# First attention layer's window phase: the next layer's group norm by ScalarE squares with sums and GpSimd two-operation pieces

## The chip, the cores and the metric

The kernel runs on one core of a Trainium2 chip. The metric is the device time of one execution in microseconds (us). TensorE is called PE in the profile, VectorE DVE, ScalarE ACT, GpSimd POOL; SP issues the DMAs.

## The reference

Four images of 256 channels and 64x64 positions pass through four layers, each added to its own input. Layers 0 and 1 are attention layers, layers 2 and 3 are state-space (Mamba) layers. Every layer's input is first normalised in 32 groups:

```python
def _gn(v, G=32, eps=1e-5):
    B_, H_, W_, C_ = v.shape
    g = v.reshape(B_, H_, W_, G, C_ // G)
    m = jnp.mean(g, axis=(1, 2, 4), keepdims=True)
    s = jnp.var(g, axis=(1, 2, 4), keepdims=True)
    return ((g - m) / jnp.sqrt(s + eps)).reshape(v.shape)
...
x = x + L0(_gn(x))   # attention
x = x + L1(_gn(x))   # attention
x = x + L2(_gn(x))   # state space
x = x + L3(_gn(x))   # state space
```

(The last four lines are shortened.) Since the array is (image, channel, row, column), its last axis, the image column, plays the part of the channel, and a group is two neighbouring columns. So a norm needs the mean and the variance of pairs of columns over all channels and rows.

An attention layer runs a gated recurrence along one image axis (the scan phase), cuts the result into 64 windows of 8x8, picks for each window the four windows with the most similar mean, and attends with 8 heads from the window's 64 queries to the 256 keys of those four (the window phase). A depthwise 3x3 convolution of the values ("lepe") is added, and a 1x1 projection gives the layer's output.

## The kernel before

One image at a time: `net_kernel` loops over four images ("batches" here), keeps the image x in SBUF as 128 partitions by 8192 fp32 values (two halves of channels), runs both attention layers in `attention_layers` and then the two state-space layers.

The attention layers cut the image into eight strips of eight columns, which is four norm groups per strip. A strip's slice of x is read as (channel half, column, row): neighbouring elements of that order lie 64 values apart in x, because columns are innermost in memory. All order within a phase is the order of the program text (`manual_schedule`): each engine runs its own instructions in that order, and waits for the others where data or a buffer demands it.

The norm of one strip has two forms.

- `gn` (L125) makes the normalised strip in seven steps: sums of x by DVE, a small product on PE that adds over channels, `center` (a DVE copy of the mean, then a GpSimd subtraction of 128x1024 into a buffer with tag "xn", L151), `square` (one ScalarE instruction of 128x1024 into a buffer with tag "sq", L156), `reduce` (a DVE sum of 128x1024, L160), a small product, and `scale` (a small DVE add, a GpSimd power, L168, and a GpSimd multiply of 128x1024 in place, L172).
- `stats` (L189) makes only the variances, for the state-space layer that follows layer 1: sums, product, negative mean, four ScalarE squares of 128x256 straight from x with the mean as bias and the sum accumulated by the same instruction (L215), product, and a small copy.

Tag "xn" has two buffers, tag "sq" has one. The one "sq" buffer also holds the products of the convolution's taps where GpSimd does them: `weigh` (L254) multiplies a shifted image by a weight into it, and `add` (L257) adds it to the value image. Each is one step, and GpSimd runs one such step per pair.

The window phase (`window_phase`, L477) loops over 32 pairs of windows. Pair i has two halves h of the heads. Per half: `scores` (PE, L546), `smallest` (DVE, L558), `exps` (four ScalarE instructions with accumulated sums, L569), `normalise` (a DVE reciprocal, L581, and four GpSimd multiplies of 128x256, L584), `turn` (eight PE transposes, L597), `turned` (one copy on DVE, L608, one on ScalarE, L610), `values` (PE, L623), and once per pair `own_rows` (a DVE add of the pair's outputs, L634). The halves and pairs are interleaved: pair i's loop body transposes the second half of pair i-1 and makes the first scores of pair i+1. In two pairs of every four, `project` adds a 1x1 projection into a finished strip of x (DVE, L644). `gather` issues the key and value loads for pair i+3 on SP's queue.

Other work is hung into this loop by two tables, `mids` and `ends`: steps under `mids[i]` run in the middle of pair i, before `normalise(i, 0)`; those under `ends[i]` at its end, behind the pair's tap. In layer 0 these are the norms of layer 1's first two strips, strip s in pairs 7+4s to 12+4s; in layer 1 they are the `stats` of strips 0 to 6:

```python
if nxt:
    load_scan_weights(nxt)
    for s in range(2):
        i = 7 + 4 * s
        plan(gn(nxt, s, lambda: psum), (ends, i), (ends, i + 1), (mids, i + 2),
             (ends, i + 3), (mids, i + 4), (ends, i + 4), (mids, i + 5))
```

Layer 1's scan phase reads the two normalised strips as the input of its first products (`conv_ps<-att_xn`).

Of the kernel before, what the change touches and what calls it, by code (L numbers as in the profile page):

```python
# [8 lines left out]
F32 = mybir.dt.float32  # L9
# [3 lines left out]
ALU = mybir.AluOpType  # L13
# [5 lines left out]
P = 128  # L19
# [4 lines left out]
NW = 8  # L24
# [20 lines left out]
class Net:  # L45
# [33 lines left out]
    def attention_layers(self, x, w_drams, v_drams):  # L79
        tc, nc = self.tc, self.nc  # L80
        with ExitStack() as ctx:
# [31 lines left out]
            def load_scan_weights(lay):  # L113
                lay["wa"] = wp.tile([P, 2, 4 * C], F32, tag="wa", name="att_wa")
                nc.sync.dma_start(lay["wa"], lay["w"][:, :, 0 : 4 * C])
# [70 lines left out]
                return g[0], both(g[1], g[2]), both(g[3], g[4]), both(g[5], g[6])  # L186


            def stats(s, psum):  # L189
                xs = x.rearrange("p (c h w) -> p c w h", c=2, w=S)[:, :, strip[s], :]  # L190
                box = {}

                def columns(tag, part):
                    box[tag] = psum().tile([P, NT], F32, tag="mm", name=f"gn_{tag}")
                    nc.tensor.matmul(box[tag][:, 0:4], self.one_gn, part, start=True, stop=True)

                def sums():
                    box["s1"] = self.small.tile([P, 4], F32, tag="gn_s1", name="gn_s1")
                    xr = x.rearrange("p (n w) -> p n w", w=S)[:, :, strip[s]]
                    nc.vector.tensor_reduce(  # L200
                        box["s1"], xr.rearrange("p n (g t) -> p g n t", t=2), AX.XY, ALU.add
                    )

                def mean():
                    box["mean"] = self.small.tile([P, 4], F32, tag="gn_mean", name="gn_mean")
                    nc.vector.tensor_scalar(
                        box["mean"], box["pm"][:, 0:4], -1.0, None, ALU.mult
                    )

                def square(g):  # L210
                    if g == 0:
                        box["s2"] = self.small.tile([P, 4], F32, tag="gn_s2", name="gn_s2")
                        box["sq"] = norm.tile([P, 2, 8, S], F32, tag="xn", name="gn_sq")
                    two = slice(2 * g, 2 * g + 2)
                    nc.scalar.activation(  # L215
                        box["sq"][:, :, two], xs[:, :, two], AF.Square,
                        bias=box["mean"][:, g : g + 1], accum_out=box["s2"][:, g : g + 1],
                    )

                def variance():  # L220
                    nc.vector.tensor_copy(self.gvar[:, 4 * s : 4 * s + 4], box["pv"][:, 0:4])  # L221

                return (
                    sums, lambda: columns("pm", box["s1"]), mean,
                    *(lambda g=g: square(g) for g in range(4)),
                    lambda: columns("pv", box["s2"]), variance,
                )


# [247 lines left out]
            def window_phase(lay, work, psum, idx, nxt, taps):  # L477
# [13 lines left out]
                def load_row():  # L491
                    listed = dram.tile([NW * NW, 8], U32, tag="listed", name="listed")
                    nc.sync.dma_start(listed, idx)
                    nc.sync.dma_start(
                        row.rearrange("o (s a) k -> o s a k", a=NW),
                        listed[:, 0:TOPK].rearrange("(o a s) k -> o s a k", o=1, a=NW),
                    )
# [37 lines left out]
                def scores(i, h):  # L535
                    sj, a = divmod(i, 4)
                    if i < n_pair:
                        sc[h] = psum.tile([P, 2, 2, 2, P], F32, tag="sc", name="sc", bufs=2)
                        for w in range(2):
                            for m in range(2):  # L540
                                for b in range(2):
                                    for r in range(2):
                                        r0 = r * 64 + h * 32
                                        rows = slice(r0, r0 + 32)
                                        k0 = b * P + m * 64
                                        nc.tensor.matmul(  # L546
                                            sc[h][b * 64 : b * 64 + 64, r, w, m, :],
                                            (own(sj, m) if r == b else swap[sj % 2][:, m])[
                                                rows, 2 * a + w
                                            ],  # L550
                                            kv[i, w][rows, :, k0 : k0 + 64],
                                            start=True, stop=True,
                                        )
# [98 lines left out]
                for i in range(3):  # L652
                    gather(i)
                    indices(i + 1)
                load_row()
                scores(0, 0)
                scores(0, 1)
                early = [query(lay, 5, m, psum, nc.vector, tag="pt", bufs=2) for m in range(2)]
# [5 lines left out]
                mids, ends, left = {}, {}, []  # L664

                def plan(steps, *where):
                    for f, (at, i) in zip(steps, where):
                        if i < n_pair:
                            at.setdefault(i, []).append(f)
                        else:  # L670
                            left.append(f)

                if nxt:
                    load_scan_weights(nxt)
                    for s in range(2):
                        i = 7 + 4 * s
                        plan(gn(nxt, s, lambda: psum), (ends, i), (ends, i + 1), (mids, i + 2),
                             (ends, i + 3), (mids, i + 4), (ends, i + 4), (mids, i + 5))
                else:

                    for s in range(NW - 1):
                        i = 4 * s + 7
                        plan(stats(s, lambda: psum), (ends, i), (ends, i + 1), (mids, i + 2),
                             (ends, i + 2), (mids, i + 3), (ends, i + 3), (mids, i + 4),
                             (ends, i + 4), (mids, i + 5))
                for i in range(n_pair):
                    sj, a = divmod(i, 4)
                    add = evict = None
# [63 lines left out]
                box = {}  # L752
# [3 lines left out]
            with tc.tile_pool(name="at_p0", bufs=2, space=PSUM, reuse_waits="tile") as psum:  # L756
                box = {"psum": psum}
                g = [gn_four(layers[0], s, lambda: box["psum"]) for s in range(2)]
# [3 lines left out]
            for i, lay in enumerate(layers):  # L762
                with tc.tile_pool(name=f"at_a{i}", bufs=1, reuse_waits="tile") as work, tc.tile_pool(
                    name=f"at_p{i}", bufs=5, space=PSUM, reuse_waits="tile"
# [1407 lines left out]
```

## Time and profile before

| | |
|---|---|
| median of 3 runs | 11914.07 us (11912.61 to 11917.38) |
| profiled execution | 11903.13 us, span 11901.3 us, mean granted TensorE clock 0.932 |
| PE busy | 10069.9 us (85%) |
| DVE busy | 9868.8 us (83%) |
| POOL busy | 8695.6 us (73%) |
| ACT busy | 7006.9 us (59%) |

In the profile a row such as "L156 ACT ACTIVATE gn_sq<-att_xn 128x1024 x64: 1046/1056/1057" is one group of instructions: source line, engine, operation, output and inputs, shape, number, and the shortest, median and longest duration in ns. Timeline rows begin with the start and the duration in us; the square brackets give the time for which the engine sat idle before the row, and what released it. Rows of windows begin with a stretch of time and its length, then the busy time of each engine with its number of instructions, then the TensorE clock that was granted (1.00 is full speed), the share of time that the DMA engines were busy, and what they moved.

### The profile page before, as it was taken

To read this page: it belongs to the slowest core of one execution; us is meant where nothing else is said; L and a number is where in the kernel's file an instruction comes from. 1 tells how busy PE (TensorE), PEld (TensorE's weight loads), DVE (VectorE), ACT (ScalarE), POOL (GpSimd) and SP (SyncE) were. 2 spreads that over 40 slices of the span, in tenths; PEclk is the share of its full clock that TensorE was granted. 3 is DMA by queue.
4 is the path that set the end of the run, shared out by engine and by line. 5 is a ranking of instruction groups with operands and counts; after the bars stand their busy time and mean duration, and the time that the engine had idled before them with its cause. 6 is when DMAs were issued, how large, how long until landed. Compare 5 with 4: busy or idle time off the path is not lost. (4 is left out here: it accounts for less than half of the span.)

```text
span 11901.3 us, 192225 instructions
## 1 busy us (share of the span) xinstructions
PE 10069.9 (85%) x71104; PEld 5762.7 (48%) x71104; DVE 9868.8 (83%) x8422; ACT 7006.9 (59%) x13096; POOL 8695.6 (73%) x5918
## 2 busy tenths in 40 slices
PE   8998887777899888777789988877778998887777
PEld 4564454444456455444445645544444564554444
DVE  6677998998767799899866779989987677998998
ACT  4565554776456555577645655557764565555776
POOL 4566886898456688689845668868984566886897
PEclk9998998999999899899999989989999998998998
DMA  3344454554334455455433445545543344554554
GB/s 96 101 133 137 173 178 144 171 181 159 89 99 137 138 172 175 147 169 181 157 88 101 133 139 172 176 147 169 181 158 92 98 134 139 173 175 145 169 175 154
DMA packets 682505, 1742.09 MB, mean 146 GB/s; under 512 B 88896, under 2 KB 194896, under 8 KB 681312
## 3 DMA queue, kind: packets, MB, share of 16 engines
q1 hardware_dynamic: 676448, 1721.41, 44.7%
q8 instruction: 563, 9.22, 0.3%
q10 hardware_dynamic: 5120, 8.39, 0.3%
q14 instruction: 374, 3.06, 0.1%
HBM read 1601.52 MB, written 94.39 MB: 142 GB/s over the span
## 5 line engine op out<-in xcount | busy, mean ns | idle before, releaser
L1016 POOL TENSOR_TENSOR hc<-h,cb 128x1024 f32<-128x1024 f32 x2056 | 4807.7, 2350 | 785.6 <-DVE h L1010 341.4
L1010 DVE TENSOR_TENSOR_SCAN h<-da,m_state,pb 128x1024 f32<-128x1024 f32 x1248 | 2920.2, 2340 | 163.1 <-DVE pb L1004 4.3
L962 PE MATMUL y<-ident,hc 128*128 128x128 f32 x16384 | 2345.2, 290 | 404.4 <-POOL hc L1016 333.7
L962 PEld LDWEIGHTS y<-ident,hc 128*128 128x128 f32 x16384 | 2043.7, 150 | 1127.6 <-POOL hc L1016 575.0
L1004 DVE TENSOR_TENSOR pb<-du,pb 128x1024 f32<-128x1024 f32 x1672 | 2024.4, 1211 | 118.9 <-PE pb L934 116.8
L946 ACT ACTIVATE da<-delta,m_v 128x1024 f32<-128x1024 f32 x1672 | 1899.4, 1141 | 135.7 <-DVE h L1010 118.9
L934 PE MATMUL pb<-m_parts,pick 128*128 128x512 bf16 x3312 | 1081.8, 411 | 835.0 <-DVE h L1010 768.7
L584 POOL TENSOR_SCALAR pr<-pr,sm,zero 128x256 f32<-128x256 f32 x2048 | 1136.1, 569 | 533.6 <-DVE sm L581 530.2
L569 ACT ACTIVATE pr<-sc,mn 128x256 f32<-128x256 f32 x2048 | 952.7, 477 | 552.4 <-DVE sm L581 359.9
L934 PEld LDWEIGHTS <-pick 128*128 128x128 bf16 x3312 | 264.0, 101 | 1779.8 <-DVE h L1010 977.2
L558 DVE TENSOR_REDUCE mn<-sc 128x4 f32<-128x1024 f32 x512 | 629.6, 1231 | 528.3 <-PE sc L546 527.0
L1010 DVE TENSOR_TENSOR_SCAN h<-da,pb 128x1024 f32<-128x1024 f32 x424 | 969.3, 2286 | 55.6 <-ACT m_u L1704 0.5
L920 POOL TENSOR_TENSOR bb<-du,bb 128x1024 f32<-128x1024 f32 x376 | 888.5, 2363 | 118.7 <-DMA bb<-m_cd 108.3
L597 PE MATMUL pt_ps<-ident,pr 128*128 128x128 f32 x4096 | 663.9, 297 | 85.0 <-POOL pr L584 40.2
L1010 DVE TENSOR_TENSOR_SCAN h<-dap,m_state,bb 128x1024 f32<-128x1024 f32 x288 | 672.2, 2334 | 65.9 <-ACT dap L946 46.1
L233 PE MATMUL conv_ps<-att_y,att_wb 128*128 128x512 f32 x1536 | 686.7, 597 | 3.0 <-DVE gvar L221 3.0
L546 PE MATMUL sc<-kv,q_swap 32*64 32x128 f32 x8192 | 599.4, 286 | 11.4 <-DMA kv<-kv_dram 8.8
L946 ACT ACTIVATE dap<-delta,m_v 128x1024 f32<-128x1024 f32 x376 | 419.8, 1116 | 308.5 <-DVE h L1010 245.8
L546 PE MATMUL sc<-kv,att_y 32*64 32x128 f32 x7168 | 580.1, 287 | 17.4 <-DMA kv<-kv_dram 13.7
L597 PEld LDWEIGHTS pt_ps<-ident,pr 128*128 128x128 f32 x4096 | 471.5, 148 | 225.6 <-POOL pr L584 138.4
L271 DVE SCALAR_TENSOR_TENSOR lp<-vimg,att_v,lp 128x512 f32<-128x512 f32 x672 | 507.7, 755 | 30.8 <-DVE lp L271 1.0
L546 PEld LDWEIGHTS sc<-kv,att_y 32*64 32x64 f32 x7168 | 434.0, 139 | 153.3 <-issue 58.8
(300 smaller groups left out, 17799.4 us busy)
## 6 DMA issues: line engine op xcount, KB each, us to landing
cb<-m_cd SPq DMA_DIRECT2D x2048, 512.0 KB, 3.8
kv<-kv_dram SPq DMA_DIRECT2D x1984, 128.0 KB, 2.8
bb<-m_cd SPq DMA_DIRECT2D x376, 512.0 KB, 5.5
kv_dram<-kst SPq DMA_DIRECT2D x128, 256.0 KB, 3.9
kv_dram<-vn SPq DMA_DIRECT2D x128, 256.0 KB, 4.1
q_swap<-att_y SPq DMA_DIRECT2D x96, 256.0 KB, 4.4
m_pe<-in_pe_dram SPq DMA_DIRECT2D x32, 512.0 KB, 4.5
out_dram<-yo SPq DMA_DIRECT2D x64, 256.0 KB, 2.4
```

The costliest lines, as they stand in the source:

```text
L233: nc.tensor.matmul(ps, w[:, k, w0 + m * P : w0 + (m + 1) * P], src[:, k], start=(k == 0), stop=(k == 1),)
L546: nc.tensor.matmul(sc[h][b * 64 : b * 64 + 64, r, w, m, :], (own(sj, m) if r == b else swap[sj % 2][:, m])[rows, 2 * a + w], kv[i, w][rows ...
L569: nc.scalar.activation(t[:, g].rearrange("p j r t -> p r j t"), sc[h][:, :, g // 2, g % 2, :].rearrange("p r (j t) -> p r j t", j=2), AF.E ...
L584: nc.gpsimd.tensor_scalar(t[:, g], t[:, g], s[:, g : g + 1], self.zero, ALU.mult, ALU.add)
L597: nc.tensor.transpose(pt[h][j][:, g, :], t[:, g, j].rearrange("p r t -> p (r t)"), self.ident,)
L920: nc.gpsimd.tensor_tensor(pb[i], slots[i][0]["du"], pb[i], ALU.mult)
L934: nc.tensor.matmul(pb[i][:, ss], self.pick[:, n : n + 1].to_broadcast([P, P]), blk["parts"][:, ss], start=True, stop=True,)
L946: nc.scalar.activation(da[i], blk["delta"], AF.Exp, scale=blk["a"](n))
L962: nc.tensor.matmul(blk["y"][:, ss], t[:, ss], self.ident, is_transpose=True, start=(n == 0 and ss.start % NT == 0), stop=(n == DS - 1 and ...
L1004: nc.vector.tensor_tensor(pb[i], blk["du"], pb[i], ALU.mult)
L1010: nc.vector.tensor_tensor_scan(h[i][:, ss], da[i][:, ss], pb[i][:, ss], state, ALU.mult, ALU.add)
L1016: nc.gpsimd.tensor_tensor(hc[i][:, ss], h[i][:, ss], cb[i][:, ss], ALU.mult)
```

## The change

`stats` gets a parameter `lay`. Where it is given, the tile that the squares are written to is registered as the next layer's normalised strip, and two kinds of step take the place of the copy of the variance: `deviation` (a small DVE add and a GpSimd power) and `scale` (GpSimd, two pieces of 128x256, each adding the negative mean to x and multiplying by the reciprocal deviation in one instruction, into the tile that held the squares). Layer 0's window phase uses it for both strips in place of `gn`, over pairs 7+4s to 14+4s; layer 1's use of `stats` has the same steps and places as before. The load of the next layer's weights stands earlier in the text.

```diff
-            def stats(s, psum):
+            def stats(s, psum, lay=None):
...
                         box["sq"] = norm.tile([P, 2, 8, S], F32, tag="xn", name="gn_sq")
+                        if lay:
+                            lay["xn"][s] = box["sq"]
...
+                def deviation():
+                    rstd = self.small.tile([P, 8], F32, tag="gn_rstd", name="gn_rstd")
+                    box["rstd"] = rstd = rstd[:, 0:4]
+                    nc.vector.tensor_scalar(rstd, box["pv"][:, 0:4], 1e-5, None, ALU.add)
+                    nc.gpsimd.tensor_tensor(
+                        rstd, rstd, self.minus_half.to_broadcast([P, 4]), ALU.pow
+                    )
+
+                def scale(*gs):
+                    for g in gs:
+                        two = slice(2 * g, 2 * g + 2)
+                        nc.gpsimd.tensor_scalar(
+                            box["sq"][:, :, two], xs[:, :, two], box["mean"][:, g : g + 1],
+                            box["rstd"][:, g : g + 1], ALU.add, ALU.mult,
+                        )
+
                 return (
                     sums, lambda: columns("pm", box["s1"]), mean,
                     *(lambda g=g: square(g) for g in range(4)),
-                    lambda: columns("pv", box["s2"]), variance,
+                    lambda: columns("pv", box["s2"]),
+                    *((deviation, lambda: scale(0, 1), lambda: scale(2, 3)) if lay else (variance,)),
                 )
...
                 load_row()
+                if nxt:
+                    load_scan_weights(nxt)
                 scores(0, 0)
...
-                if nxt:
-                    load_scan_weights(nxt)
-                    for s in range(2):
-                        i = 7 + 4 * s
-                        plan(gn(nxt, s, lambda: psum), (ends, i), (ends, i + 1), (mids, i + 2),
-                             (ends, i + 3), (mids, i + 4), (ends, i + 4), (mids, i + 5))
-                else:
...
+                for s in range(2 if nxt else NW - 1):
+                    i = 4 * s + 7
+                    plan(stats(s, lambda: psum, nxt), (ends, i), (ends, i + 1), (mids, i + 2),
+                         (ends, i + 2), (mids, i + 3), (ends, i + 3), (mids, i + 4),
+                         (ends, i + 4), (mids, i + 5), (ends, i + 6), (ends, i + 7))
```

More of the change, by code (lines that the diff above doesn't have):

```diff
@@ L671, in plan @@
                             left.append(f)
-                if nxt:
-                    load_scan_weights(nxt)
-                    for s in range(2):
-                        i = 7 + 4 * s
-                        plan(gn(nxt, s, lambda: psum), (ends, i), (ends, i + 1), (mids, i + 2),
-                             (ends, i + 3), (mids, i + 4), (ends, i + 4), (mids, i + 5))
-                else:
[L681 to L685, printed above, removed]
+                for s in range(2 if nxt else NW - 1):
[3 more added lines that the diff above has]
+                         (ends, i + 4), (mids, i + 5), (ends, i + 6), (ends, i + 7))
                 for i in range(n_pair):
```

## The prediction

> **What bounds the kernel now.** I read the page first: over the whole span no engine is full (PE 85%, DVE 83%, POOL 73%), and the chain that ended last names only later layers. So it can't price an edit in the first attention layer's window phase (the loop over 32 pairs), and I timed the pairs there. Each pair has one DVE add at L634; from pair 8's to pair 17's are nine pairs, and all steps of the changed norm but the first and the last fall in them. In the four batches that stretch takes 88.57, 89.67, 86.31 and 86.96 us in layer 0 (sum 351.5). Layer 1 runs the same loop, but its norm steps at these pairs are `stats` (sums, mean, four ScalarE squares) instead of `gn`: 64.42, 65.38, 64.42 and 65.87 us (sum 260.1). The table of windows shows batch 0: layer 0's stretch, layer 1's, and two later pairs of layer 0 with no norm in them.
>
> ```profile
> core 0: us, PE busy (x) PEld busy (x) DVE busy (x) ACT busy (x) POOL busy (x), PEclk, DMA share, GB/s
> 300.14:388.71 88.57, 77.22 (x1327) 57.82 (x1327) 50.80 (x80) 45.44 (x164) 61.44 (x87) 0.75 0.45 130
> 763.17:827.59 64.42, 61.56 (x1329) 45.45 (x1329) 48.70 (x80) 49.99 (x180) 49.43 (x81) 1.00 0.60 166
> 388.71:403.15 14.44, 14.16 (x299) 10.01 (x297) 10.57 (x18) 10.25 (x37) 10.57 (x18) 1.00 0.50 147
> ```
>
> Undisturbed, a pair is 7.22 us and TensorE is busy for 14.16 of 14.44: TensorE is the bound. In layer 0's stretch it has the same work, yet is busy 15.7 us longer, at a granted clock of 0.75, and idle 8.5 us longer (11.35 against 2.86): 24.2 us in all. The timeline shows where it starts, first on ScalarE, then TensorE by window:
>
> ```profile
> 313.73 0.22 ACT L569 ACTIVATION_READ_ACCUMULATOR pr<-sc,mn 128x1 f32 x1
> 318.85 1.06 ACT L156 ACTIVATE gn_sq<-att_xn 128x1024 f32<-128x1024 f32 x1 [4.89 <-POOL vimg L257]
> 319.81 0.46 ACT L569 ACTIVATE pr<-sc,mn 128x256 f32<-128x256 f32 x1
> ```
>
> ```profile
> core 0: us, PE busy (x), PEclk, DMA share, GB/s
> 317.00:320.00 3.00, 0.73 (x8) 1.00 0.47 131
> 320.00:323.00 3.00, 1.65 (x16) 0.72 0.69 205
> 323.00:326.00 3.00, 3.00 (x92) 0.50 0.13 42
> ...
> 334.00:335.00 1.00, 0.00 (x0) 0.99 0.39 131
> 335.00:336.00 1.00, 0.47 (x1) 0.50 0.54 123
> ```
>
> The square writes the one buffer (tag "sq") that GpSimd's taps use too, so it waits for the tap add of its own pair, queued behind that pair's normalising. All exps stand behind it on ScalarE, so no scores get free, TensorE starves and its clock halves.
>
> A second stall is on GpSimd, at pair 12: the power and the 128x1024 multiply stand ahead of the pair's normalising, whose output TensorE transposes.
>
> ```profile
> 330.81 1.64 POOL L168 TENSOR_TENSOR gn_rstd<-gn_rstd,minus_half 128x8 f32<-128x8 f32 x1 [1.61 <-DVE sm L581]
> 332.53 1.90 POOL L172 TENSOR_TENSOR att_xn<-att_xn,gn_rstd 128x1024 f32<-128x1024 f32 x1
> 334.42 4.74 POOL L584 TENSOR_SCALAR pr<-pr,sm,zero 128x256 f32<-128x256 f32 x8
> ```
>
> TensorE waits 2.24 us there, and the clock is 0.50 from 335 to 345. Pair 13 then takes 14.63 us, against 7.82 in layer 1.
>
> **The change, part by part.** It concerns two strips in each of four batches: eight strips.
>
> ```profile
> L215 ACT ACTIVATE gn_sq<-x,gn_mean x128: 707/758/797, 768.9 to 9867.5; 128x256 f32<-128x256 f32 x128
> L156 ACT ACTIVATE gn_sq<-att_xn x64: 1046/1056/1057, 18.8 to 9529.4; 128x1024 f32<-128x1024 f32 x64
> L160 DVE TENSOR_REDUCE gn_s<-gn_sq x64: 1212/1219/1221, 19.9 to 9533.9; 128x4 f32<-128x1024 f32 x64
>   POOL vimg L257: 38.9, 8
> ...
> L151 POOL TENSOR_TENSOR att_xn<-x,gn_mean x64: 2457/2466/2476, 16.3 to 9526.9; 128x1024 f32<-128x1024 f32 x64
> L172 POOL TENSOR_TENSOR att_xn<-att_xn,gn_rstd x64: 1899/1901/1902, 23.8 to 9544.1; 128x1024 f32<-128x1024 f32 x64
> L584 POOL TENSOR_SCALAR pr<-pr,sm,zero x2048: 544/555/1082, 238.1 to 9852.4; 128x256 f32<-128x256 f32 x187
> ```
>
> Removed: the wait for the taps (38.9 us, 8 times, 4.9 each), the 1.06 square, the 1.22 DVE sum, and GpSimd's subtraction (2.47) and multiply (1.90). Added on ScalarE: four squares; in layer 1's timeline one holds the engine 0.87 us with its accumulator read (801.36 to 802.23), so 3.5 us, 2.4 more than before. They write an "xn" buffer, free since the scan phase, and wait only for the mean. ScalarE's 49.99 busy of 64.42 in layer 1's stretch contains all this; beyond layer 1's time it costs nothing, and if ScalarE were last, 8 x 2.4 = 19.5 us. DVE's and TensorE's small steps keep their places. The load of the next weights moves in the text only: SP issues nothing in between, so it passes no DMA, and no gather is later: 0.
>
> Taking layer 1's measured time for the stretch therefore gives 351.5 - 260.1 = **91.4 us** less. From it goes what layer 1 does not do:
>
> The power (pairs 12 and 16): 1.64 us, the same instruction at half the width, taken unchanged. It waits for DVE's small add, as now, and the pair's normalising is queued behind it. In layer 1 pair 12's first normalising runs from 788.70 to 790.86 and its eight transposes from 791.01 to 792.10. The power would start at 788.5, so normalising ends at 792.3 and the transposes about 0.9 late; the second normalising starts 1.0 late, and its transposes already wait for it. TensorE has no slack after that: 1.1 us, times 8 is 8.8. Bounds: 0 (the subtraction before pair 9's normalising, 2.47 us, left that pair at 7.83 in both layers) to 1.64, 13 us in all.
>
> The pieces: GpSimd TENSOR_SCALAR 128x256, the form of L584 (0.555), but reading x at a step of 64 elements. No row has both. L151 reads x so, L172 does not: 0.565 us on 1024 elements, 0.14 on 256, so 0.70 a piece, 1.40 a pair of pieces. [...] The first two pieces stand after pair 13's tap (ends 802.08 in layer 1): the next normalising ends at 805.64, before its transposes at 805.86: nothing. The second two after pair 14's tap (809.69): normalising starts 1.32 late, ends at 813.25, its transposes (812.42 to 813.51) slip by 0.4, the second normalising by 0.45 and its transposes with it: 0.45, times 8 is 3.6. Bounds: 0 to 1.4 a pair of pieces with no cover, 22 us.
>
> Sum: 91.4 - 8.8 - 3.6 = 79.0 us. Against the profiled execution, whose span is 11901.3 (1.8 us less than its time of 11903.13), that is a span of 11822.3. The median shown, 11914.07, is 10.9 above that execution; the same 79.0 off it gives **11835 us**.
>
> **The clock decides the size.** Without it only the idle part, 8.5 us a batch or 34 us, would come back. [...] I still take it as warm: in layer 1 between 716 and 803 the emptiest 3 us after the start held 2.38 us of TensorE work at a clock of 1.00, and the new waits come in parts of about 1 us.
>
> **Rivals.**
> Cold again (13%): the power's two delays fall where TensorE is busy 2.45 of 3 us (788 to 791) and may leave some 1.6, as in 320 to 323, where the clock fell. Each such pair would cost 14.63 - 7.82 = 6.8: eight of them 54 us, leaving 25; half of them leave about 52. Time 11862 to 11889.
> Wholly hidden (10%): power and pieces disappear as the subtraction at pair 9 did, and layer 0 has no third strip's sums in these pairs: 91 to 99 us, 11815 to 11823.
> It does not do what it says (6%): another wait takes the tap's place, so that TensorE still starves, within 24 us of 11914. For it: ScalarE's exps wait for DVE in both layers. Against: in layer 1's stretch the same squares start without a wait.
> Slower (5%): GpSimd's pieces are dear. They stand ahead of a normalising 16 times. If a piece costs 1.7 us or more, a pair of pieces of 3.4 less 1.1 of slack makes TensorE wait 2.3 us, which cooled it at 335: 6.8 each, 16 x 6.8 = 109 us against 91.4, so 17 us slower or more, 11931. It decides from 1.7 a piece, 2.4 times my value; L254, a TENSOR_SCALAR with short rows at 0.77 for 512 elements, speaks against.
> What is as forecast, 79 give or take 16, has the other 66%.
>
> **How the numbers follow.** A measurement of this kernel tells about 0.2%, 24 us, from no change. Faster by more: 66 + 10 + 13 = 89%; within: 6%; slower: 5%. The range runs from wholly hidden (11815) to all pairs but a few cold (11885) and leaves out the last two cases.
>
> **What would show it.** Right: the stretch from pair 8 to 17 in layer 0 at about 68 us and clock 1.00 in all batches; no wait of a square for the taps; 32 more squares of 128x256, 8 fewer of L156, L160, L151 and L172; 32 pieces near 0.70; TensorE's wait at pair 12 near 1 us. Wrong: the clock at 0.5 around pairs 12 to 13 (power) or 14 to 16 (pieces), a piece above 1.1 us, or pairs outside 9 to 19 that got longer.

## The result, and the profile after

| | before | after |
|---|---|---|
| median | 11915.72 us (11912.61 to 11921.65, 4 runs) | 11814.67 us (11809.23 to 11830.3, 4 runs) |
| profiled execution | 11903.13 us (span 11901.3) | 11818.82 us (span 11817.0) |
| granted clock, whole span | 0.932 | 0.937 |
| PE busy | 10069.9 us | 9974.1 us |
| layer 0's window phase, first pair's add to the last's, four batches | 982.1 us | 896.1 us |
| stretch pair 8 to pair 17 in it, four batches | 351.5 us | 264.7 us |

The ratio is 0.9917 (95% interval 0.99 to 0.9934): 101 us less in the medians. The profiled executions differ by 84.3 us. Layer 0's window phase alone is 86.0 shorter, so outside it there is neither a gain nor a price to speak of. The two differences, 101 and 84.3, don't agree because the profiled execution of before was 12.6 us under its median and that of after 4.1 over (84.3 + 12.6 + 4.1 = 101.0).

The first view is the table of windows of the changed kernel, with the columns of the one shown for before: layer 0's stretch in batch 0, layer 1's, and two pairs of layer 0 after the stretch.

```profile
core 0: us, PE busy (x) PEld busy (x) DVE busy (x) ACT busy (x) POOL busy (x), PEclk, DMA share, GB/s
298.95:364.28 65.33, 60.48 (x1327) 44.69 (x1327) 47.47 (x78) 49.19 (x178) 54.77 (x87) 1.00 0.59 167
739.32:803.14 63.82, 60.10 (x1329) 44.86 (x1329) 48.79 (x81) 49.89 (x180) 49.69 (x81) 1.00 0.60 170
364.11:378.57 14.46, 14.16 (x298) 10.02 (x297) 10.56 (x17) 10.25 (x37) 13.48 (x22) 1.00 0.61 173
```

The stretch was 88.57 us. TensorE does the same 1327 products in 60.48 us instead of 77.22, at a clock of 1.00 instead of 0.75, and its idle time is 65.33 - 60.48 = 4.85 us instead of 11.35. So of 23.2 us less in this batch 16.7 are the clock and 6.5 the waits. GpSimd's count grew by four in the third row's two pairs: the second strip's pieces fall there, and the two pairs still take 14.46.

ScalarE's timeline, where the square had waited 4.89 us, and below it GpSimd's and TensorE's around pair 12 and at the pieces:

```profile
312.11 0.49 ACT L588 ACTIVATE pr<-sc,mn 128x256 f32<-128x256 f32 x1
...
312.56 0.80 ACT L217 ACTIVATE gn_sq<-x,gn_mean 128x256 f32<-128x256 f32 x1
...
314.09 0.47 ACT L588 ACTIVATE pr<-sc,mn 128x256 f32<-128x256 f32 x1 [0.65 <-DVE sm L600]
```

```profile
324.38 1.02 POOL L229 TENSOR_TENSOR gn_rstd<-gn_rstd,minus_half 128x4 f32<-128x4 f32 x1 [0.75 <-DVE sm L600]
325.39 4.76 POOL L603 TENSOR_SCALAR pr<-pr,sm,zero 128x256 f32<-128x256 f32 x8
...
338.36 1.55 POOL L236 TENSOR_SCALAR gn_sq<-x,gn_mean,gn_rstd 128x256 f32<-128x256 f32 x2
...
345.99 1.56 POOL L236 TENSOR_SCALAR gn_sq<-x,gn_mean,gn_rstd 128x256 f32<-128x256 f32 x2
```

```profile
326.79 0.63 PE L616 MATMUL pt_ps<-ident,pr 128*128 128x128 f32 x3
327.63 0.76 PE L616 MATMUL pt_ps<-ident,pr 128*128 128x128 f32 x5 [0.21 <-POOL pr L603]
```

The squares stand between exps and wait for nothing. The power stands where it stood, 0.62 us shorter, and the multiply behind it is gone. TensorE's wait for the normalising of pair 12, 2.24 us before, is 0.21.

The groups of the tiles that the steps write, with minimum, median and maximum in ns:

```profile
L217 ACT ACTIVATE gn_sq<-x,gn_mean x160: 707/761/800, 304.7 to 9777.1; 128x256 f32<-128x256 f32 x160
...
L156 ACT ACTIVATE gn_sq<-att_xn x56: 1047/1056/1057, 19.0 to 9444.0; 128x1024 f32<-128x1024 f32 x56
L160 DVE TENSOR_REDUCE gn_s<-gn_sq x56: 1211/1220/1222, 20.1 to 9448.5; 128x4 f32<-128x1024 f32 x56
L236 POOL TENSOR_SCALAR gn_sq<-x,gn_mean,gn_rstd x32: 777/788/806, 338.4 to 9231.2; 128x256 f32<-128x256 f32 x32
...
L229 POOL TENSOR_TENSOR gn_rstd<-gn_rstd,minus_half x8: 1018/1018/1027, 324.4 to 9209.1; 128x4 f32<-128x4 f32 x8
```

There are 32 more small squares and 8 fewer of each large step, as the diff says, and the squares' wait for the taps (`vimg`, 38.9 us, 8 times) has no row any more. The two new prices are a piece, 0.788 us, and the power on four columns, 1.02 us.

### The profile page after: what moved, and what is told of

It is laid out like the page before. It is cut to its first block, busy times and chain, and to the rows that moved or that the text cites. A ratio compares the mean times of both kernels' runs of the same rounds, so it can differ in the third digit from the quotient of the medians.

```text
span 11817.0 us, 191849 instructions
## 1 busy us (share of the span) xinstructions
PE 9974.1 (84%) x70632; PEld 5725.4 (48%) x71104; DVE 9859.5 (83%) x8414; ACT 7022.2 (59%) x13152; POOL 8688.2 (74%) x5934
## 4 chain that ended last, share of the span: by engine, by line
PE 37%; DVE 34%; ACT 11%; issue 8%; POOL 6%; DMA 2%; SPq 1%; DVEq 0%; POOLq 0%; ACTq 0%; another core or an unknown queue 0%
DVE h L1023 18%; PE conv_ps L252 9%; DVE pb L1017 7%; PE y L975 6%; PE u_ps L1312 4%; POOL pr L603 3%; PE sc L565 2%; DVE lp L290 2%; ACT da L959 2%; PE pb L947 2%; PE u_ps L1685 2%; PE pt_ps L616 2%; POOL hc L1029 1%; PE z_ps L1337 1%; ACT dap L959 1%
## 5 line engine op out<-in xcount | busy, mean ns | idle before, releaser
L947 PE MATMUL pb<-m_parts,pick 128*128 128x512 bf16 x2840 | 971.5, 413 | 826.5 <-DVE h L1023 765.5
L1023 DVE TENSOR_TENSOR_SCAN h<-dap,m_state,bb 128x1024 f32<-128x1024 f32 x288 | 672.2, 2334 | 69.1 <-ACT dap L959 47.8
```

Of the source, the lines that this page charges most:

```text
L947: nc.tensor.matmul(pb[i][:, ss], self.pick[:, n : n + 1].to_broadcast([P, P]), blk["parts"][:, ss], start=True, stop=True,)
L1023: nc.vector.tensor_tensor_scan(h[i][:, ss], da[i][:, ss], pb[i][:, ss], state, ALU.mult, ALU.add)
```

## The experiments

The theory: two stalls, the shared taps' buffer and the multiply ahead of the normalising, each starve TensorE for a few microseconds, and the half clock that follows is most of the price. The rivals: only one of the two matters; the cheaper form of the norm matters, not its buffer or place; the stalls cost their idle time and the clock is a bystander. The kernels are versions of before or after with one thing changed (in e9_cover three places), after_again is the changed kernel itself, and none leaves work out. "Phase" is layer 0's window phase summed over four batches, "stretch" its pairs 8 to 17. Each ratio is to the kernel before, timed on the same chip; beside the three groups of runs it took 11910.3, 11908.48 and 11907.04 us, so medians of different groups can be compared to a few us.

| run | edit | stretch, us | phase, us | median, us | ratio (95%) |
|---|---|---|---|---|---|
| before | | 351.5 | 982.1 | | |
| e1_buffer | before, squares in a free buffer | 302.4 | 935.1 | 11857.32 | 0.9954 (0.994 to 0.9969) |
| e2_place | before, multiply at the pair's end | 317.9 | 942.0 | 11883.7 | 0.9973 (0.9963 to 0.9983) |
| e3_both | both | 272.7 | 900.5 | 11836.0 | 0.9938 (0.9921 to 0.9954) |
| e5_fill | before, useless products on TensorE | 318.5 | 954.1 | 11877.71 | 0.9965 (0.9951 to 0.9979) |
| after | | 264.7 | 896.1 | 11814.67 | 0.9917 (0.99 to 0.9934) |
| after_again | after, timed once more | 269.8 | 897.8 | 11819.75 | 0.9925 (0.9911 to 0.9938) |
| e4_taps_buffer | after, squares in the taps' buffer | 305.1 | 925.0 | 11861.05 | 0.9962 (0.9949 to 0.9974) |
| e6_pieces_mid | after, pieces in the middle of pairs 12 and 16 | 312.5 | 936.1 | 11855.59 | 0.9961 (0.9948 to 0.9973) |
| e7_power_end | after, power at a pair's end | 261.2 | 888.3 | 11813.66 | 0.9927 (0.9909 to 0.9944) |
| e8_twice | after, each piece twice | 284.3 | 935.8 | 11836.2 | 0.9945 (0.9928 to 0.9963) |
| e9_cover | after, power and pieces at other pairs | 262.4 | 898.3 | 11815.53 | 0.992 (0.9906 to 0.9933) |

### The old form without its two stalls

The buffer alone: the large square writes a free strip of `y` instead of tag "sq".

```diff
+                    if free is not None:
+                        box["sq"] = free
...
-                        plan(gn(nxt, s, lambda: psum), (ends, i), (ends, i + 1), (mids, i + 2),
+                        free = y[:, :, strip[0], :].rearrange("p c w h -> p c (w h)")
+                        plan(gn(nxt, s, lambda: psum, free=free), (ends, i), (ends, i + 1), (mids, i + 2),
```

> The kernel before, with one edit: in the window phase the square of gn writes into strip 0 of y, which is idle there, instead of the buffer that it shares with the taps. The stretch from pair 8 to pair 17 of layer 0, summed over the four batches, is 351.5 us before and 264.7 after the change. Theory, the two stalls pay separately: pairs 11 and 15 fall from 11.0 to about 6.1, pairs 13 and 17 stay at 13 to 14; stretch about 312, time about 39 us under before. Rival, one stall feeds the other (the clock that the square cools is what makes the power and multiply dear): pairs 13 and 17 fall too, stretch about 280, some 70 us under before. Rival, only the GpSimd stall counts: stretch above 340.

The place alone: the multiply becomes a step of its own at the end of pair i+6; the power stays.

```diff
-                    nc.gpsimd.tensor_tensor(xn, xn, wide(rstd), ALU.mult)
+                    box["rstd"] = rstd
+
+                def multiply():
+                    nc.gpsimd.tensor_tensor(xn, xn, wide(box["rstd"]), ALU.mult)
...
-                             (ends, i + 3), (mids, i + 4), (ends, i + 4), (mids, i + 5))
+                             (ends, i + 3), (mids, i + 4), (ends, i + 4), (mids, i + 5), (ends, i + 6))
```

> The kernel before, with one edit: gn's GpSimd multiply of 128x1024 (1.90 us) moves from the middle of pair i+5, ahead of the normalising, to the end of pair i+6; the power stays. The square still waits for the taps. Theory, separate stalls: pairs 11 and 15 stay at 11.0, pairs 13 and 17 fall from 13 to 14 to about 8.5 to 9; stretch about 300, time about 50 us under before. Rival, one stall feeds the other: with the clock cold from pair 11 on, pairs 12, 13, 16 and 17 stay together above 19 us each two; stretch above 325, less than 27 us under before.

Both edits together:

> The kernel before with both edits, the square's own buffer and the later multiply, and still gn's form: one subtraction, one square of 128x1024, one DVE sum. Theory, buffer and place are all that counts and the form of squares and pieces is free: stretch 264 to 272, time 80 to 90 us under before, like the changed kernel. Rival, the form counts (GpSimd has 4.4 us of norm work a strip here against 4.2, DVE 1.2 more, the power 1.64 instead of 1.02): stretch above 285.

Measured: the buffer takes 49.1 us from the stretch, the place 33.6, both 78.8, so they nearly add (82.7). In time e1_buffer is 53 us faster than the kernel before beside it, e2_place 27, e3_both 74. The buffer gave more than expected (a stretch of 302.4 for 312) and the place less (317.9 for 300); but pairs 13 and 17 stay at 13 to 14 us in e1_buffer, so the rival that one stall feeds the other falls. Each stall matters, and only a small rest is the form: in undisturbed batches the stretch is 66.6 to 67.0 us in e3_both and 65.3 in the changed kernel, some 5 to 7 us over four batches. In time that rest can't be told (0.9938 against 0.9917 and 0.9925, with overlapping intervals). The rival that the new form itself is the main gain falls. The moved load of the next weights has no run of its own; e3_both, which leaves it where it was, has nearly the whole gain, so it can't be worth much.

What each stall is worth is not its wait. In e1_buffer the multiply still stands at pair 12, and TensorE still waits 2.18 us there. Its windows, then its whole stretch in batch 0:

```profile
core 0: us, PE busy (x), PEclk, DMA share, GB/s
325.00:328.00 3.00, 1.59 (x75) 1.00 0.69 195
328.00:331.00 3.00, 1.54 (x5) 0.80 0.41 133
331.00:334.00 3.00, 3.00 (x40) 0.50 0.66 175
```

```profile
298.66:374.18 75.52, 67.05 (x1327) 49.45 (x1327) 50.34 (x80) 45.82 (x164) 61.64 (x87) 0.91 0.54 152
```

The clock falls to 0.50 behind that wait, and the stretch's clock is 0.91. Pair 13 is 13.0 to 14.0 us, against 8.3 in the changed kernel.

In e2_place the size depends on something finer. The program is the same in each batch, but pair 17 took 11.91 us in batch 0 and 8.75 in batch 1. Here, as throughout the traces of before and after, the clock changes only at points that lie whole multiples of 3.413 us apart. TensorE's windows on that grid where pair 17 begins, batch 0 and then batch 1:

```profile
core 0: us, PE busy (x), PEclk, DMA share, GB/s
364.91:368.32 3.41, 2.06 (x56) 1.00 0.43 130
368.32:371.73 3.41, 3.41 (x40) 0.50 0.58 170
371.73:375.15 3.42, 3.42 (x10) 0.50 0.77 226
375.15:378.56 3.41, 3.41 (x104) 1.00 0.07 18
```

```profile
3334.48:3337.90 3.42, 2.47 (x77) 1.00 0.39 110
3337.90:3341.31 3.41, 2.92 (x46) 1.00 0.65 172
```

In batch 0 the waits fall into one window, which is left with 2.06 us of work, and the next two run at half clock. In batch 1 they are shared by two windows with 2.47 and 2.92, and the clock stays at 1.00. With the same program pair 17 took 3.2 us more in the batch where the waits fell into one window.

### Keeping TensorE busy through the stalls

The kernel before, with useless products (identity times a strip of `y`, into an unused accumulator) ahead of the transposes that come late.

```diff
+                def fill(n):
+                    t = psum.tile([P, NT], F32, tag="mm", name="fill_ps")
+                    for _ in range(n):
+                        nc.tensor.matmul(t, self.ident, y[:, 0, 0:8, :].rearrange("p c h -> p (c h)"),
+                                         start=True, stop=True)
...
                 def turn(i, h):
+                    if nxt and h == 0 and i in (12, 16):
+                        fill(4)
...
+                        if nxt and h and j and i in (10, 14):
+                            fill(6)
```

> The kernel before with nothing taken away: filler products of 128x512 whose result nobody reads stand where TensorE waits: six between the two halves of the transposes of pair 10 and 14 (second half of heads), four ahead of the first transposes of pairs 12 and 16, in layer 0; 20 a batch, about 0.45 us each at full clock, 36 us in all. Theory, the granted clock makes most of the loss: the fill lies in idle time, the clock stays at 1.00, and the kernel gets faster though it does more: stretch about 310, time about 40 us under before. Rival, the waits alone cost and the clock is a symptom: stretch 352 to 390, not faster than before.

The fill was twice the size I meant: each fp32 product shows as two records (x12 for six), and the two places of a strip took 5.32 and 3.70 us.

```profile
317.68 5.32 PE L593 MATMUL fill_ps<-att_y,ident 128*128 128x512 f32 x12
...
332.39 3.70 PE L593 MATMUL fill_ps<-att_y,ident 128*128 128x512 f32 x8
```

```profile
299.62:379.05 79.43, 76.25 (x1367) 51.69 (x1367) 51.38 (x80) 45.62 (x164) 61.56 (x87) 1.00 0.51 145
```

So 9.02 us of products that nobody needs were added to each of eight strips, 72 us in all, and the kernel became 33 us faster (11877.71 against 11910.3; the stretch 33.0 us shorter). The waits are still there: ScalarE's first square still stands 4.90 us behind the tap. The clock is 1.00 in all four batches, and TensorE's useful work in the stretch takes 76.25 - 2 x 9.02 = 58.2 us instead of 77.2. The rival that the clock is a bystander falls.

### The change with one stall put back

The taps' buffer again: the squares write tag "sq" behind the same tap as before, and the pieces write an own "xn" tile.

```diff
-                        box["sq"] = norm.tile([P, 2, 8, S], F32, tag="xn", name="gn_sq")
+                        box["sq"] = norm.tile(
+                            [P, 2, 8, S], F32, name="gn_sq",
+                            **(dict(tag="sq", bufs=1) if lay else dict(tag="xn")),
+                        )
...
-                         (ends, i + 2), (mids, i + 3), (ends, i + 3), (mids, i + 4),
+                         *([(ends, i + 3), (ends, i + 3), (mids, i + 4), (mids, i + 4)] if nxt else
+                           [(ends, i + 2), (mids, i + 3), (ends, i + 3), (mids, i + 4)]),
```

> The changed kernel with one part undone: the four squares write the buffer that the taps use, two at the end of pair i+3 and two in the middle of pair i+4, and the pieces write a strip buffer of their own. The stretch from pair 8 to 17 of layer 0, over four batches, is 264.7 us in the changed kernel. Theory: ScalarE waits for the tap add again, about 4.9 us, and the clock falls; pairs 11 and 15 are back at about 11, what the buffer alone gave (49 us) is lost again; stretch near 314, time some 50 us over the changed kernel. Rival, with squares that read x instead of the GpSimd subtraction the shared buffer no longer hurts: stretch under 285.

The pieces where the multiply was:

```diff
-                         (ends, i + 4), (mids, i + 5), (ends, i + 6), (ends, i + 7))
+                         (ends, i + 4), (mids, i + 5), (mids, i + 5), (mids, i + 5))
```

> The changed kernel with one part undone: power and all four pieces stand in the middle of pair i+5, ahead of its normalising, where the power and multiply stood before; 1.02 + 4 x 0.79 = 4.2 us against 3.5 then. Theory, the place makes the stall: pairs 13 and 17 are back at 13 to 15 and pairs 12 and 16 at about 6.6, stretch near 306, time some 40 us over the changed kernel. Rival, GpSimd's work counts wherever it stands: no difference, stretch 260 to 272.

Both lose what the single repairs of before had won. With the taps' buffer the wait is back in its old size:

```profile
317.51 0.72 ACT L218 ACTIVATE gn_sq<-x,gn_mean 128x256 f32<-128x256 f32 x1 [4.83 <-POOL vimg L278]
```

Pairs 11 and 15 take 11.97 us (11.0 in the kernel before), the stretch is 40.4 us longer than the changed kernel's, and the median is 46 us above its 11814.67. With the pieces in the middle of the pair, GpSimd's timeline of batch 1 reads:

```profile
3283.01 1.02 POOL L229 TENSOR_TENSOR gn_rstd<-gn_rstd,minus_half 128x4 f32<-128x4 f32 x1 [0.75 <-DVE sm L600]
3284.13 3.49 POOL L236 TENSOR_SCALAR gn_sq<-x,gn_mean,gn_rstd 128x256 f32<-128x256 f32 x4
3287.61 4.32 POOL L603 TENSOR_SCALAR pr<-pr,sm,zero 128x256 f32<-128x256 f32 x8
```

Power and pieces hold up the normalising of pair 12 by 4.5 us, a little more than power and multiply did (3.5), and pair 13 takes 14.0 to 15.1 us: the stretch is 47.8 us longer, the median 41. The same pieces, at the ends of the next two pairs, cost nothing at three of their four places in a batch and 1.4 us at the fourth (below). Place and buffer make the gain.

### What the new steps cost where they stand

Three runs on the sums of the prediction. The power at a pair's end:

```diff
-                         (ends, i + 4), (mids, i + 5), (ends, i + 6), (ends, i + 7))
+                         (ends, i + 4), (ends, i + 5) if nxt else (mids, i + 5), (ends, i + 6), (ends, i + 7))
```

> The changed kernel with the power moved too: from the middle of pair i+5 to its end, behind the tap. Theory, what the change still costs in pairs 13 (8.33 against 7.82 in layer 1), 16 (7.46 against 6.84) and 17 (8.09 against 7.82) is the power ahead of the normalising; these three fall to layer 1's values, 1.4 us a batch less, stretch near 259, time about 6 us under the changed kernel, which the times can hardly tell. Rival, the same delay at another place: pairs 13 and 17 unchanged or longer, stretch 264 to 275.

Each piece twice, with the same output:

```diff
-                    for g in gs:
+                    for g in gs + gs:
```

> The changed kernel with every piece made twice (same inputs, same output), so 3.15 us of GpSimd work stands ahead of the normalising of pairs 14, 15, 18 and 19 instead of 1.58. The single pieces cost nothing (pairs 14, 15, 18, 19 at 7.23, 6.2, 7.23, 7.23). Theory, cover of 1.3 to 1.6 us: the second half lies on the path, 1.2 to 1.6 us for each of 16 places, about 22 us, no clock loss; pairs 14 to 16 and 18 to 20 together longer by about 2.8 each strip. Rival, GpSimd has room for it all: no change within 8 us. Rival, TensorE's waits get long enough to cool it: 50 us and more.

Power and pieces at pairs where TensorE's feeders seemed to have more room:

```diff
-                         (ends, i + 4), (mids, i + 5), (ends, i + 6), (ends, i + 7))
+                         (ends, i + 4), (mids, i + 5), (mids, i + 6), (ends, 13 + 8 * s), (ends, 17 + 8 * s))
```

> The changed kernel with power and pieces moved to places where the loop before hid GpSimd work: the power to the middle of pairs 13 and 17 (there the subtraction of 2.47 us at pair 9 cost nothing), the pieces to the ends of pairs 13, 17, 21 and 25 (where the first two pieces cost nothing). Theory, what the change still costs (pair 13 0.5 us, pair 16 0.6, pair 17 0.3 over layer 1's values) is place alone: pairs 13, 16 and 17 at 7.82, 6.84 and 7.82, stretch near 258, all of layer 0's window phase some 6 us shorter than in the changed kernel, a gain that the times can hardly tell. Rival, GpSimd's added 5.3 us a batch cost somewhere else: pairs 14, 18, 22 or 26 longer by 0.3 to 0.6, no gain.

And the changed kernel itself again, beside e9_cover:

> The changed kernel once more, beside the kernel above: 11810 to 11820 us; the stretch of layer 0 264 to 269 us over four batches, as the first time. It is the measure of what two equal kernels differ by: a stretch outside these would say that the pair times of one profile can't carry differences of 6 us.

Measured, as undisturbed pairs in us (layer 1 has no power and no pieces, but in pairs 16, 17 and 20 it carries further strips' steps that layer 0 does not have):

| pair | layer 1 | after | power at the end | pieces twice | other pairs |
|---|---|---|---|---|---|
| 13 | 7.82 | 8.33 | 8.55 | 8.33 | 7.82 |
| 15 | 6.11 | 6.12 | 6.11 | 6.95 | 6.11 |
| 16 | 6.84 | 7.46 | 7.46 | 12.5 | 6.10 |
| 17 | 7.82 | 8.09 | 7.64 | 8.15 | 7.64 |
| 19 | 7.22 | 7.23 | 7.21 | 8.12 | 7.22 |
| 20 | 8.57 | 7.65 | 7.65 | 12.2 | 7.64 |

With the power moved, pair 17 falls to 7.64, pair 13 rises from 8.33 to 8.55, and pair 16 stays at 7.46. So what pair 16 pays is not for the power; it goes when the pieces leave the end of pair 14 (last column).

How much it pays depends on what it is compared with. Without the pieces it is 6.10 us in layer 0 (last column, and in three batches of e6_pieces_mid too), not layer 1's 6.84: at the end of pair 15 layer 1 makes the sums of its third strip, and layer 0 has only two (pair 12, behind such sums in both layers, is 6.84 in both).

```profile
789.67 1.21 DVE L200 TENSOR_REDUCE gn_s<-x 128x4 f32<-128x1024 f32 x1
```

Against layer 0's own pairs, the second pieces cost 7.46 - 6.10 = 1.36 us at pair 16 and nothing at pair 20, and the power costs 0.51 at pair 13 and 8.09 - 7.64 = 0.45 at pair 17: 2.3 us a batch. Layer 1's pairs 16 and 17 are 0.74 and 0.18 longer than layer 0's would be, so against them it looks like 1.4. At a pair's end the power costs pair 13 somewhat more (0.73) and pair 17 nothing.

In seven of the eight batches of the changed kernel and its repeat TensorE waits some 0.7 us for the normalising behind the second pieces, and in batch 2 of the former, as in batch 1 of the repeat, the clock fell there: pair 16 took 9.15 and 9.16 us. Batch 2, first TensorE's row, then its windows of the 3.413 us grid, and last the same place in batch 0, where the clock stayed:

```profile
6250.45 0.77 PE L616 MATMUL pt_ps<-ident,pr 128*128 128x128 f32 x5 [0.70 <-POOL pr L603]
```

```profile
core 0: us, PE busy (x), PEclk, DMA share, GB/s
6249.09:6252.50 3.41, 2.50 (x43) 1.00 0.41 122
6252.50:6255.92 3.42, 3.42 (x40) 0.50 0.64 191
...
347.43:350.84 3.41, 2.25 (x60) 1.00 0.54 154
```

Doubling the pieces shows how far the cover reaches. A first pair of pieces of 3.15 us (pairs 15 and 19) costs 0.8 to 0.9; of 1.58, nothing. A second one costs 5 us at pair 16 and, in three batches of four, 4.5 at pair 20, as the clock falls behind TensorE's wait, now 1.73 us (batch 1, pair 16, first the row, then TensorE by windows of the 3.413 us grid):

```profile
3297.70 2.94 PE L616 MATMUL pt_ps<-ident,pr 128*128 128x128 f32 x8 [1.73 <-POOL pr L603]
```

```profile
core 0: us, PE busy (x), PEclk, DMA share, GB/s
3293.89:3297.30 3.41, 1.64 (x76) 1.00 0.51 147
3297.30:3300.72 3.42, 2.83 (x10) 0.50 0.66 192
...
3307.54:3310.95 3.41, 3.41 (x56) 0.50 0.42 117
```

1.6 us more of GpSimd work costs 5 us of TensorE's. This is the mechanism of the prediction's "slower" rival, at half of its places, and it shows that the changed kernel is less than 1.6 us of GpSimd work from it. The phase is 39.7 us longer. The median is 21 us above after's and 16 above after_again's, near the 22 expected, but by luck: the expectation had no clock loss in it. The rest of the program, which the edit doesn't touch, was 25 to 31 us shorter in this profile than in the two of the changed kernel, spread over all batches; why is open.

Neither move of the steps makes a faster kernel that these runs can tell. In undisturbed batches the steps at other pairs save 2.3 us each (62.9 against 65.2), as much as they cost by pair (0.51 + 1.36 + 0.45), but the profiled stretch is 262.4 and the phase 898.3, no better than after, and the median beside it is 11815.53 against 11819.75 with overlapping intervals (0.9906 to 0.9933 and 0.9911 to 0.9938). The power at the end gave 11813.66, also within the changed kernel's own spread.

The repeat shows why a profile alone is good to some 5 us here (264.7 and 269.8 for one kernel, the second just outside the 264 to 269 that I had set). Batch 1's stretch was 74.49 us while the other three had 65.22, 65.21 and 64.89. Pairs 11 to 13 took 9.1, 9.71 and 10.47: two gathers of keys came late. (Pair 16's 9.16, in the same batch, is the second pieces' loss shown above.)

```profile
3266.67 0.65 PE L565 MATMUL sc<-kv,att_y 32*64 32x128 f32 x2 [0.94 <-DMA kv<-kv_dram]
```

```profile
core 0: us, PE busy (x), PEclk, DMA share, GB/s
3262.80:3266.21 3.41, 2.19 (x24) 1.00 0.62 180
3266.21:3269.62 3.41, 2.95 (x76) 0.50 0.54 157
...
3283.28:3286.69 3.41, 3.41 (x22) 0.50 0.64 199
```

A wait of 0.60 us for a gather before 3264.76 and the first half of the one shown (3265.73 to 3266.67) left 2.19 us of work in a window of 3.41, and the clock was halved for the next six. Such waits stand in both layers of the changed kernel's first profile too: one of 0.95 us ends at 6216.8 in layer 0 and one of 1.24 at 3704.9 in layer 1, with one half-clock window from 6218.4 and one from 3706.2. So I compare single pairs in undisturbed batches, and whole kernels by their times.

## Why the prediction was right or wrong

**The direction and the mechanism were right.** Faster was given 89%. The clock of the stretch is 1.00 in three batches and 0.93 in batch 2, where it fell twice: for one window behind a late gather, and for two behind the second pieces. The wait for the taps is gone, and the stretch is 264.7 us in four batches, 66 each, where about 68 was said. e1_buffer, e2_place, e4_taps_buffer and e6_pieces_mid show the two stalls one by one from both sides; e5_fill, 33 us faster with 72 us of products added, shows that the clock makes the size.

**The time was missed by 20 us.** 11835 was forecast and 11814.67 measured, at the lower edge of the range (11815). The miss has two parts.

The first is the sum: 79.0 us forecast against 84.3 between the profiled executions, or 86.85 in the stretch. Two of its terms were mis-sized and a third was put at nothing.
- The power, "1.1 us, times 8 is 8.8", cost 0.51 at pair 13 and 0.45 at pair 17: 3.8 us over the four batches. Its duration was mis-sized by taking the eight-column row unchanged: 1.02 us on four columns against 1.64 on eight, so the width counts. And "TensorE has no slack after that" was wrong: TensorE's wait at pair 12 is 0.21 us, where near 1 was said.
- The second two pieces, "0.45, times 8 is 3.6", cost 1.36 on strip 0 and nothing on strip 1: 5.4 us, and more where the clock falls behind them. The first pair of pieces costs nothing, as said. A piece takes 0.788 us, where my 0.70 was built from two rows of before; the difference, 16 x 0.088 = 1.4 us for the second pairs, was smaller than the other errors.
- Layer 1 was taken as layer 0 without the disputed steps, but it also makes the sums of a third strip, worth 0.74 + 0.18 us a batch in pairs 16 and 17, or 3.7 in all. The forecast named this only in the rival "Wholly hidden" and put it at nothing in its own sum.

So 12.4 us of price became 9.3, and 3.7 us of gain were left out: 6.8 us, which would have made the sum 85.8. That the two mis-sized terms went in opposite ways, one too dear and one too cheap, is luck.

Apart from that third strip the stand-in, layer 1's 260.1 us, held: its undisturbed batch is now 63.82, and layer 0's is 65.3 with the new steps and 62.9 where e9_cover hides them. Late gathers moved single batches of both by 2 to 4 us.

The second part is larger. I set the forecast at 79.0 under the median of before, as if the profiled execution of after would lie under its median by as much as before's. It did not: 10.9 under the median that I had became 4.1 over, 15 us together. Timed again, the two kernels differ by 87 us (11819.75 against 11907.04), which is what the stage explains (86.0); the 101 of the first comparison has 79 to 119 as its interval. The mechanism accounts for the 86, and the rest is within what the runs can't tell.

**The clock.** I took it as warm after the change, from 2.38 us of work in 3 us of layer 1 (760 to 763) at a clock of 1.00, and nearly always it was: in batch 0 a window with 2.25 us of work keeps its clock. The exception is the second pieces, one of the signs named for being wrong (0.5 around pairs 14 to 16), in one batch of four here and one of four in the repeat, at 1.7 us each. In before's second stall, with its wait of 2.24 us, and at e8_twice's wait of 1.73 us the clock fell after windows with 1.19 and 1.64 us of work. The fixed grid of 3.413 us on which all this lies shows in the trace of before, and I should have laid the new waits over it.

**The rivals.** "Cold again" did not come, since the power's delay is 0.2 at TensorE and not two of 1. "Wholly hidden" is the nearest of them in time (11815 to 11823), but only half in mechanism: 9.3 us of new steps are visible, while the squares and the pieces of pair 13 are hidden, and its point about the third strip's sums holds. "It does not do what it says" and "slower" were wrong for this kernel. The latter's mechanism is real: it put the point at 1.7 us a piece, and 1.58 a piece (each done twice) already made TensorE wait 1.73 us and cost 5 us, but only behind the second pieces, and behind the first 0.8 to 0.9. Behind the second pieces TensorE waits 0.70 us for 1.58 us of work and 1.73 for 3.15, a slack of 0.9 to 1.4: the forecast's 1.1 us per pair of pieces was about right there, and the "16 times" was not.

## What to carry to other kernels

Price a wait of the engine that bounds a loop by what its clock does afterwards: two stalls per strip, of 4.9 us on ScalarE and 2.2 on TensorE, cost 86 / 8 = 10.8 us here, and the same loop in another layer, without them, was the best measure of it. Don't let a step write a buffer that another engine's queue of side work holds, when what feeds the bounding engine stands behind that step (ScalarE's exps here, behind the 4.9 us), and don't put side work ahead of the instruction that feeds the bounding engine (here 3.5 us of power and multiply, for the 2.2); at the end of a pair, behind the feed, the same pieces cost between nothing and 1.4 us. When a sister loop is taken as the measure, list what else it does: here a third strip's sums hid 3.7 us. When a forecast is made on one profiled execution and judged on medians, that execution's own distance from its median (here 4 to 13 us) belongs into the range.

## What the runs showed of the hardware

- The granted clock was 1.00 or 0.50, and its changes lie on a fixed grid of 3.413 us: in the clock records of before and after every stretch at one clock but the last, 491 and 479 of them, lasts a whole multiple of 3413.33 ns to within 1 ns. Batch 0 of the kernel before, by windows of the grid:

```profile
core 0: us, PE busy (x), PEclk, DMA share, GB/s
317.91:321.32 3.41, 0.43 (x4) 1.00 0.60 167
321.32:324.73 3.41, 3.38 (x52) 0.50 0.47 143
324.73:328.15 3.42, 3.42 (x70) 0.50 0.32 79
328.15:331.56 3.41, 3.41 (x86) 1.00 0.59 180
331.56:334.97 3.41, 1.19 (x64) 1.00 0.31 97
334.97:338.39 3.42, 2.74 (x10) 0.50 0.55 146
```

- The windows before a fall were not idle. Both layers' window phases of before and after, laid on that grid, hold 960 windows at full clock, and the clock fell after 40 of them, with 0.43 to 2.88 us of TensorE work by the profile's busy time. It fell after all 16 with under 1.9 us of work, after none of the 821 with over 2.9, and after 24 of the 123 between (2.25 us kept it and 2.50 lost it at the same place of the changed kernel). In after_again the window of 2.19 us before the fall held no gap longer than 0.60 us; the longest two were 0.60 and 0.48.
- Once lost, the clock stayed at 0.50 for two windows in e1_buffer (329.8 to 336.6), three in before (335.0 to 345.2), four in e8_twice (3297.3 to 3310.9), six in after_again (3266.2 to 3286.7) and eight in before (358.9 to 386.2), although TensorE was busy for most of that time (24.3 us of the last 27.3). At 0.50 a window full of work costs up to 3.413 / 2 = 1.7 us, by my estimate from these records.
- How long it stayed goes with what filled the windows. In the same window phases of before and after 79 half-clock windows were full of TensorE work (over 3.3 of 3.413 us). Where the score products (weights of 32x64, against 128x128 for transposes and projections) took under 0.75 us of the window, the clock came back after all 30; where they took 1.3 us or more, it stayed at 0.50 after 35 of 36; in between it came back after 8 of 13. The eight windows of before ended with one that held projection products and transposes alone. No run was made to test this, so it is an association, and the cause is open.
- Useless products in TensorE's waits paid for themselves in e5_fill: 72 us of them made the kernel 33 us faster.
- A GpSimd power took 1.02 us on 128x4 (after) and 1.64 on 128x8 (before). A two-operation piece of 128x256 that reads with a step of 64 elements took 0.788 us (after), against 0.555 for the same kind of instruction on neighbouring elements (before).
